# Setup of a two-direction graph attention kernel: key bursts over four PSUM banks become bursts over six, with a new order of the work between them

## The chip, the cores and the metric

The kernel runs on one core of one Trainium2 chip. The metric is device time in microseconds of one execution. TensorE is called PE here (PEld is its weight loading), VectorE DVE, ScalarE ACT, GpSimd POOL and SyncE SP. SP issues most DMAs, in the order of the program.

## The reference, cut to what matters

For each of B = 16 batches with N = 512 nodes and F = 512 features, each node attends, in two directions d, to the first 20 nodes of its batch, in 16 heads of 32 features:

```python
self_feat = concat([v, q_exp], -1) @ W_self.T + b_self
output = self_feat
for d in range(2):
    kv = self_feat[:, :20]
    qh = (self_feat @ Wq[d].T + bq[d]).reshape(B, N, 16, 32)
    kh = (kv @ Wk[d].T + bk[d]).reshape(B, 20, 16, 32)
    aff = einsum('bnhd,bmhd->bnhm', qh, kh) / sqrt(32)
    w = softmax(where(cond > 0, aff, NEG) + label_bias)
    out_t = einsum('bnhm,bmf->bnhf', w, kv)
    output = output + einsum('bnhf,hgf->bnhg', out_t, Wout[d]) + bout[d]
result = v + relu(output)
```

`cond` and `label_bias` are sums over 11 labels of an integer adjacency array, read one way for d = 0 and transposed for d = 1.

## The kernel before, in words

The kernel has a setup and a loop over the batches. All products are in fp32, and a matmul has two records in the trace, one for each of two passes. The order of the instructions is written out by hand on every engine (`manual_schedule`), so each engine and each DMA queue works through its own list in the order of the program.

**What setup makes.** It computes the features of the 20 attended nodes of all batches (`kvn`, 128 partitions by 4 blocks of features by 320), takes the first node of each batch from the other 19 (`kvD`, 16 x 19 = 304 columns, L822), and multiplies by Wk (`key_rows`, L839), which gives `khD`, one block of 304 columns for each direction d and group of four heads hg. Then `keys` (L938) multiplies each head's 32 rows of Wq with its `khD`, which turns the keys into vectors over the 512 features, so that the loop can take scores from `self_feat` alone. These are the **key bursts**. The whole is 4 blocks of features fc x 4 groups hg x 2 directions x 304 columns = 9,728 columns for each of four heads hl.

**A burst before.** The columns of a block stand as (batch, node). A burst takes 25 or 26 batches of 19 columns, 475 or 494 columns, in two or three runs, where a run ends at a change of fc, hg or d. The four heads hl lie on four groups of 32 partitions, so their matmuls (tile 32*128) run side by side, each into a PSUM bank of its own; two tiles of two banks, `ps_g..0` (heads 0 and 1) and `ps_g..1` (heads 2 and 3). ACT evicts the first pair (L960) and DVE the second (L962), both scaled, one instruction for each run, into the stage tile `st` of its (fc, hg). There are 20 bursts. Only one set of the four banks exists, so a burst begins when the last one's are evicted, and PE has other work in between, the **fillers**.

**Stages.** A stage tile holds both directions of one (fc, hg), 608 columns a head. Those of hg 0 to 2 share three buffers in turn, those of hg 3 have one. When a stage is full, POOL copies its first two batches to `gg` (L965) and SP writes the rest to DRAM (`g_d`, 1,064 KB, L968); both must be done before the buffer is used for a new stage.

**Fillers.** Letters in a plan name them:
- k: `key_rows` of a further (d, hg), four steps of four matmuls of 304 columns, with DVE's eviction to `khD` (L848)
- m: `bias_terms`, DVE alone (L856)
- b, c: `biases` (L862, L864) and `bias_scores` (L874: four matmuls of 304 columns, ACT's copy L879, POOL's addition L883 and four stores L885 to `cq_d`)
- v, w: one step k of `values` (L901): four matmuls of 512 columns, tiles of 128*32; after the fourth step `value_pieces` evicts on DVE (L917) and stores on POOL's queue (L921)
- n: `row_flags` (L220: four matmuls of 512 columns, then DVE L222)
- p: `block_product`, one of seven products (L282, 16 records of 246 columns) that give the first batch's `self_feat`, with DVE's `partial` (L295) or `joined` (L305)

Other work is placed by the number n of the burst: mask products, counts and sums of the first batch (`mask_mul` L321 and L322, `mask_count` L330 and L331, `mask_sum` L336, `mask_spread` L344), `row_sums` on POOL (L213, L215), `x_sum` on POOL (L255), `spill` (copies in DRAM from `vw_d` to `bd_d`, L191), and loads. `load_cq(0)` (L127) reads what both `bias_scores` have stored. The loop begins with `seed_a`, `seed_d` (L425, L429), which write to the banks of the last burst, and `score_product` (L395).

Of the kernel before, what the change touches and what calls it, by code (L numbers as in the profile page):

```python
# [18 lines left out]
def gat_kernel(  # L19
# [47 lines left out]
    def bank(name):  # L67
        return acc["pool"].tile([P, 512], F32, tag="acc", name=name)
# [188 lines left out]
    def product(b, n):  # L257

        w, x = {
            1: ((0, 0), lambda: x_block(b, 0, 0)),  # L260
            2: ((0, 1), lambda: x_block(b, 1, 0)),
            3: (3, lambda: x_block(b, 1, 1)),
            4: ((1, 1), lambda: sums[b, 4]),
            5: (0, lambda: sums[b, 1]),
            6: (1, lambda: sums[b, 2]),
            7: (2, lambda: sums[b, 3]),
        }[n]
        x = x()
        home = "d" if n == 2 else "c" if n in (3, 5) else "a"
        first, last = n in (1, 2, 5), n in (2, 3, 4)  # L270
        if first:
            parts[b, home] = bank(f"ps_{home}{b}")
        for i in range(2):
            for k in range(2):
                for a in range(2):
                    at = i * P + a * P // 2
                    if isinstance(w, tuple):
                        lhs = ws_v[:, 2 * w[1] + k, bass.ds(w[0] * F // 2 + at, P // 2)]
                    else:
                        lhs = ws_s[:, w, k, bass.ds(at, P // 2)]  # L280
                    to = parts[b, home][bass.ts(a, P // 2)]
                    nc.tensor.matmul(  # L282
                        to[:, bass.ts(i, HN)], lhs, x[:, k], start=first and i + k == 0,
                        stop=last and i + k == 2, skip_group_check=True,
                    )
# [411 lines left out]
    with tc.tile_pool(name="setup", bufs=1) as sp, tc.tile_pool(name="ps_acc", bufs=4, space=PSUM) as acc["pool"]:  # L697
# [18 lines left out]
        with tc.tile_pool(name="setup_k", bufs=1) as sk:  # L716
# [17 lines left out]
            warm = bank("ps_warm")  # L734
# [36 lines left out]
            load_x(1)  # L771
            load_adj(0, 1)
# [5 lines left out]
            kv_ps = [bank(f"ps_kv{fc}") for fc in range(C)]  # L778
# [32 lines left out]
            for fc in range(C):  # L811
# [11 lines left out]
                    kvD[:, fc].rearrange("p (b m) -> p b m", m=ND), each[:, :, 1:],  # L823
# [8 lines left out]
            def key_rows(d, jc, ks=range(C)):  # L832

                if ks[0] == 0 and (d, jc) not in of:
                    of[d, jc] = bank(f"ps_k{d}{jc}")
# [32 lines left out]
        with tc.tile_pool(name="setup_g", bufs=3) as sg:  # L868

            def bias_scores(d):  # L870

                ps = bank(f"ps_c{d}")
                for c in range(C):
# [7 lines left out]
                    ps[:, : B * ND].rearrange("p (b m) -> p b m", m=ND),  # L881
# [10 lines left out]
            def values(t, ds, k):  # L892
# [3 lines left out]
                if k == 0:  # L896
                    held[1 + t // 2] = bank(f"ps_v{t}{ds[0]}")
                ps = held[1 + t // 2]
                for i, d in enumerate(ds):
                    for a in range(rows // R):  # L900
                        nc.tensor.matmul(  # L901
                            ps[bass.ds(i * rows + a * R, R)], kvT[:, k, bass.ds(t * P + a * R, R)], wo_sb[d][:, k],
# [26 lines left out]
            def keys(runs):  # L929


                pairs = [ps_s.tile([P, 2, 512], F32, tag=f"s{i}", name=f"ps_g{runs[0]}{i}", bufs=1) for i in range(2)]
                at = 0
                for fc, hg, d, lo, hi in runs:
                    n = (hi - lo) * ND
                    for hl in range(HL):
                        r = bass.ts(hl, DH)
                        nc.tensor.matmul(  # L938
                            pairs[hl // 2][:, hl % 2, at : at + n], wq_sb[r, d, hg, bass.ts(fc, P)],
                            khD[r, d * C + hg, lo * ND : hi * ND], start=at == 0, stop=True, skip_group_check=True,  # L940
                        )
                    at += n
                if not units and runs is bursts[-1]:
                    for hl in range(HL):
                        r = bass.ts(hl, DH)
                        nc.tensor.matmul(
                            pairs[hl // 2][:, hl % 2, at:], wq_sb[r, 0, 0, :P], khD[r, 0, : 512 - at],
                            start=False, stop=True, skip_group_check=True,
                        )
                at = 0  # L950
                for fc, hg, d, lo, hi in runs:
                    n = (hi - lo) * ND
                    if (fc, hg) not in stages:
                        stages[fc, hg] = (late if hg == C - 1 else sg).tile([P, B, HL, 2, ND], F32, tag="st", name=f"st{fc}{hg}")
                    st = stages[fc, hg]
                    for half in range(2):
                        to = st[:, lo:hi, bass.ts(half, 2), d].rearrange("p b h m -> p h b m")
                        of = pairs[half][:, :, at : at + n].rearrange("p h (b m) -> p h b m", m=ND)
                        if half == 0:
                            nc.scalar.activation(to, of, AF.Copy, scale=SCALE)  # L960
                        else:
                            nc.vector.tensor_scalar(to, of, SCALE, None, ALU.mult)  # L962
                    at += n
                    if d == 1 and hi == B:
# [25 lines left out]
            plan = "mmvv bvv vvc vvc vvn vvw vw vw wn p p p p p p p".split()  # L990

            units = [(fc, hg, d, b) for fc in range(C) for hg in range(C) for d in range(2) for b in range(B)]
            bursts = []
            while units:
                runs = []
                for fc, hg, d, b in units[: 25 + (len(bursts) % 5 < 3)]:
                    if runs and runs[-1][:3] == (fc, hg, d):
                        runs[-1] = (*runs[-1][:4], b + 1)
                    else:
                        runs.append((fc, hg, d, b, b + 1))  # L1000
                del units[: 25 + (len(bursts) % 5 < 3)]
                bursts.append(runs)
            rest = [(d, hg) for hg in range(C) for d in range(2)]
            first = None
# [8 lines left out]
            for n, runs in enumerate(bursts):  # L1013
                for i in range(len(rest)):
                    if (i < 1 and n > 0) or any(fc == 0 and (d, hg) == rest[0] for fc, hg, d, _, _ in runs):
                        key_rows(*rest.pop(0))
                if n in (3, 4):
                    values(*steps["v"].pop(0)[1])
# [4 lines left out]
                keys(runs)  # L1023
                if n == 8:
                    mask_count(0, 0)
                if n == 14:
                    mask_count(0, 1)
                if n == 17:
                    mask_sum(0, 1)
                value_pieces()  # L1030
                if rest:
                    for kind in "mm" if n else ():
                        f, args = steps[kind].pop(0)
                        f(*args)
                    continue
                if n == 7:
                    mask_mul(0, 0)
                first = n if first is None else first
                for kind in plan[n - first] if n - first < len(plan) else ():
                    f, args = steps[kind].pop(0)  # L1040
                    f(*args)
                    if kind == "w":
                        value_pieces()
                if n == first:
                    for d in range(2):
                        nc.gpsimd.tensor_add(br_sb, br_sb, bo_rows[d])
                if n > first:
                    value_pieces()
                if n == 10:
                    mask_sum(0, 0)  # L1050
                    load_cq(0)
                if n == 9:
                    row_sums(1)
                    copies = blocks(0)
                if n > 13:
                    spill(1, nc.gpsimd)
                    spill(1)
                if n == 11:
                    mask_mul(0, 1)
                    new_self(0)  # L1060
                    for i in range(1, 5):
                        x_sum(0, i)
                if 10 < n < 15:
                    mask_spread(0, 0, (n - 11,))
                if n == 16:
# [3 lines left out]
                if n == 18:  # L1069
# [361 lines left out]
```

## Time and profile before

| | us |
|---|---|
| median of three runs (547.0 to 547.4) | 547.39 |
| the profiled execution | 547.86 |
| its span on the core | 546.2 |
| PE busy in the span | 539.7 |
| DVE, ACT, POOL busy | 482.4, 404.5, 451.0 |
| start of the first key burst | 24.25 |
| start of the loop's first score product | 89.86 |

The profile page gives, for one execution, each engine's busy time, the span in 40 slices, the DMA queues, the chain of work that ended last, the costliest groups of instructions and the DMA issues. A group's row has the source line, the engine, output and inputs, shape and count, then busy time and the mean of one, then the idle time ahead of it with what ended it. Ends of matmuls are modelled, so a busy PE is not PE at its peak. Where a number of the text is a time of day it counts from the start of the span.

### The profile page before, as it was taken

To read this page: it belongs to the slowest core of one execution; us is meant where nothing else is said; L and a number is where in the kernel's file an instruction comes from. 1 tells how busy PE (TensorE), PEld (TensorE's weight loads), DVE (VectorE), ACT (ScalarE), POOL (GpSimd) and SP (SyncE) were. 2 spreads that over 40 slices of the span, in tenths; PEclk is the share of its full clock that TensorE was granted. 3 is DMA by queue.
4 is the path that set the end of the run, shared out by engine and by line. 5 is a ranking of instruction groups with operands and counts; after the bars stand their busy time and mean duration, and the time that the engine had idled before them with its cause. 6 is when DMAs were issued, how large, how long until landed. Compare 5 with 4: busy or idle time off the path is not lost.

```text
span 546.2 us, 19842 instructions
## 1 busy us (share of the span) xinstructions
PE 539.7 (99%) x8012; PEld 421.6 (77%) x8012; DVE 482.4 (88%) x716; ACT 404.5 (74%) x1000; POOL 451.0 (83%) x454
## 2 busy tenths in 40 slices
PE   9999999999999999999999999999999999999996
PEld 5544368889888878787888878887878788878784
DVE  1786678889999999999989999999999999999997
ACT  1225436898887979888888888887878787978564
POOL 2557996779989797979898989898998979797675
PEclk9999999999999999999999999999999999999998
DMA  8998799656766867777766757575766676736025
GB/s 298 377 400 324 260 365 352 235 172 183 233 218 182 226 204 210 234 213 231 209 219 186 244 174 246 179 235 179 222 212 203 203 216 189 234 93 192 1 65 194
DMA packets 94603, 120.30 MB, mean 220 GB/s; under 512 B 19201, under 2 KB 62783, under 8 KB 92465
## 3 DMA queue, kind: packets, MB, share of 16 engines
q1 hardware_dynamic: 93088, 116.69, 66.6%
q0 software_dynamic: 992, 1.57, 1.4%
q8 instruction: 63, 1.03, 0.8%
q10 hardware_dynamic: 432, 0.79, 0.4%
q14 instruction: 28, 0.22, 0.1%
HBM read 83.41 MB, written 36.90 MB: 220 GB/s over the span
## 4 chain that ended last, share of the span: by engine, by line
PE 89%; DMA 4%; DVE 3%; SPq 1%; ACT 1%; issue 0%; POOL 0%; DVEq 0%; POOLq 0%; ACTq 0%
PE ps_f L665 32%; PE ps_a L395 24%; PE ps_c L395 11%; PE ps_d L395 6%; PE ps_o_f L567 5%; PE ps_v L901 2%; DMA wk<-in_wkT 2%; DMA wo<-in_woT 1%; PE ps_a L282 1%; PE ps_o_c L567 1%; DMA xkv<-in_xkvT 1%; PE ps_l L395 1%; DVE bqt L856 1%; PE ps_c L282 1%; DVE st L962 1%
## 5 line engine op out<-in xcount | busy, mean ns | idle before, releaser
L325 ACT ACTIVATE prod<-adj,wb_sb 128x80 f32<-128x80 int32 x330 | 116.1, 430 | 0.0
L535 POOL TENSOR_TENSOR w<-w,sm 128x640 f32<-128x640 f32 x63 | 80.2, 1273 | 30.5 <-DVE sm L531 28.7
L665 PE MATMUL ps_f<-t,ws_s 128*64 128x246 f32 x720 | 80.0, 370 | 0.0
L665 PEld LDWEIGHTS ps_f<-t,ws_s 128*64 128x64 f32 x720 | 51.7, 136 | 18.9
L526 ACT ACTIVATE w<-w 128x640 f32<-128x640 f32 x60 | 43.9, 731 | 17.9 <-DVE w L522 17.9
L543 DVE STREAM_TRANSPOSE wt<-w 128x640 f32<-128x640 f32 x63 | 52.5, 833 | 0.1
L665 PE MATMUL ps_f<-x,ws_v 128*64 128x246 f32 x480 | 52.4, 371 | 0.0
L530 DVE TENSOR_REDUCE sm<-w 128x32 f32<-128x640 f32 x63 | 51.1, 811 | 1.1 <-ACT w L526 0.9
L521 DVE TENSOR_REDUCE ps_d<-w 128x32 f32<-128x640 f32 x59 | 48.7, 826 | 1.8 <-ACT ps_d L429 0.2
L522 DVE TENSOR_TENSOR w<-w,ps_d 128x640 f32<-128x640 f32 x59 | 48.4, 820 | 2.0
L665 PEld LDWEIGHTS ps_f<-x,ws_v 128*64 128x64 f32 x480 | 34.7, 137 | 13.0
L368 POOL TENSOR_TENSOR k<-gg,k 128x608 f32<-128x608 f32 x30 | 44.6, 1487 | 0.0
L395 PEld LDWEIGHTS ps_a<-gg,sf 128*64 128x64 f32 x544 | 34.2, 137 | 5.9 <-issue 5.8
L395 PE MATMUL ps_a<-gg,sf 128*64 128x152 f32 x544 | 38.6, 295 | 0.0
L395 PE MATMUL ps_d<-gg,sf 128*64 128x152 f32 x544 | 37.9, 293 | 0.0
L336 DVE TENSOR_REDUCE add<-prod 128x80 f32<-128x960 f32 x32 | 36.7, 1146 | 0.2 <-POOL prod L331 0.2
L344 ACT COPY both<-add 64x80 f32<-64x80 f32 x128 | 32.6, 255 | 5.7 <-DVE add L336 4.6
L567 PE MATMUL ps_o_c<-wt,ve 32*32 32x256 f32 (+1 forms) x480 | 35.9, 386 | 0.0
L680 POOL TENSOR_TENSOR t<-x,t 128x492 f32<-128x492 f32 x30 | 34.9, 1162 | 1.2
L395 PEld LDWEIGHTS ps_d<-gg,sf 128*64 128x64 f32 x544 | 35.3, 137 | 0.2 <-ACT sf L683 0.2
L680 POOL TENSOR_TENSOR t<-x 128x492 f32<-128x492 f32 x30 | 34.5, 1149 | 0.0
L197 ACT ACTIVATE xn<-xn 128x512 f32<-128x512 f32 x56 | 34.5, 619 | 0.0
(310 smaller groups left out, 1490.9 us busy)
## 6 DMA issues: line engine op xcount, KB each, us to landing
g_d<-st SPq DMA_DIRECT2D x16, 1064.0 KB, 8.5
gg<-g_d SPq DMA_DIRECT2D x56, 304.0 KB, 3.1
out_T<-o SPq DMA_DIRECT2D x60, 256.0 KB, 2.8
x<-in_xT SPq DMA_DIRECT2D x56, 256.0 KB, 4.1
xn<-in_xn SPq DMA_DIRECT2D x48, 256.0 KB, 3.8
adj<-in_adj SPq DMA_DIRECT2D x52, 220.0 KB, 2.9
nz<-nz_d SPq DMA_DIRECT2D x14, 256.0 KB, 4.5
adj<-in_adj SPq DMA_DIRECT2D x6, 440.0 KB, 7.7
```

Of the source, the lines that this page charges most:

```text
L325: nc.scalar.activation(p[:, :, l], a[:, :, l], AF.Identity, scale=wb_sb[:, l : l + 1])
L368: done["ksum"] = engine.tensor_sub(to, one, two)
L395: nc.tensor.matmul(slot(g)[bass.ts(p, P // 2), : HL * S].rearrange("p (h m) -> p h m", m=NG)[:, :, 1:], of(k)[:, bass.ds(first + g * P // ...
L521: nc.vector.tensor_reduce(mx, f, AX.X, ALU.max)
L522: done["weigh"] = (engine or nc.vector).tensor_sub(f, f, mx.unsqueeze(2).to_broadcast([P, per, NG]))
L526: done["exp"] = nc.scalar.activation(t, t, AF.Exp)
L530: nc.vector.tensor_reduce(sm, heads(weighs[b, c, l]), AX.X, ALU.add)
L535: done["normal"] = nc.gpsimd.tensor_mul(f, f, smalls.pop((b, c, l)).unsqueeze(2).to_broadcast([P, per, NG]))
L543: done["turn"] = nc.vector.transpose(wts[b][:, c, l], weighs.pop((b, c, l)).rearrange("p g w -> p (g w)"))
L567: nc.tensor.matmul(outsum[b][a][bass.ds(at // 2 * DH, n * DH), bass.ds(c * N // 2 + lo * R, (hi - lo) * R)].rearrange("p (n r) -> p n r", ...
L665: nc.tensor.matmul(parts[b][n in (2, 3, 5)][bass.ts(a, P // 2), bass.ts(i, HN)], lhs, x[:, k], start=False, stop=k == 1, skip_group_check= ...
L680: done["xsum"] = nc.gpsimd.tensor_sub(to, one, two)
```

## The change

- The columns of `kvD`, and with it of `khD` and the bursts, now stand as (node, batch). A unit is one node of 16 columns (608 units), so that runs are cut at any node.
- A burst takes six banks: `ps_g..0` for heads 0 and 2 and `ps_g..1` for heads 1 and 3 take 30 to 32 units, 480 to 512 columns a head; two further banks (`t2`, "shared") take 11 or 16 units more, 256 columns of each of two heads in a bank. There are 13 bursts, all but one of 46 to 48 units. A matmul covers 96 columns or more.
- Even heads do their shared part first, odd heads last, so that no two heads write to one bank at a time; a `nop` on PE ahead of an odd head's shared part waits for the even head's. The matmuls of the four heads are issued in the order of the columns done so far.
- ACT evicts the shared part of all four heads and the own part of heads 0 and 2, DVE the own part of heads 1 and 3. A read from PSUM now steps by 16 columns, and the write in `st` is in runs of 6 to 19 nodes.
- The four accumulation banks in turn become two fixed ones, `acc0` and `acc1`, and the shared pair, which also serves two of the four `ps_kv`.
- `values` and `row_flags` use tiles of 64 columns, two matmuls where there were four.
- A new plan of the fillers by burst; `key_rows` are in it. Loads of the second batch and half a mask (`load_x(1)`, `load_adj(0, 1)`) go behind bursts 1 and 2 on SP's queue; all twelve early spills are on SP (six were on POOL's queue), two behind each of bursts 6 to 11; `row_sums(1)` is behind burst 5, `load_cq(0)` behind burst 7.
- The last burst's padding matmuls (L946) are gone.

The core of the diff:

```diff
-        ps = bank(f"ps_nz{b}")
-        for a in range(HL):
-            nc.tensor.matmul(ps[bass.ts(a, R), :N], ones[:, :R], rss[b], start=True, stop=True)
+        ps = bank(f"ps_nz{b}", 1)
+        for a in range(2):
+            nc.tensor.matmul(ps[bass.ts(a, P // 2), :N], ones[:, : P // 2], rss[b], start=True, stop=True)
...
-            load_x(1)
-            load_adj(0, 1)
...
-                    kvD[:, fc].rearrange("p (b m) -> p b m", m=ND), each[:, :, 1:],
+                    kvD[:, fc].rearrange("p (m b) -> p b m", b=B), each[:, :, 1:],
...
-                    for a in range(rows // R):
+                    for a in range(2 * rows // P):
                         nc.tensor.matmul(
-                            ps[bass.ds(i * rows + a * R, R)], kvT[:, k, bass.ds(t * P + a * R, R)], wo_sb[d][:, k],
+                            ps[bass.ds(i * rows + a * P // 2, P // 2)], kvT[:, k, bass.ds(t * P + a * P // 2, P // 2)], wo_sb[d][:, k],
...
+            def keys(n):
+
+                runs = bursts[n]
+                pairs = [ps_s.tile([P, 2, 512], F32, tag=f"s{i}", name=f"ps_g{n}{i}", bufs=1) for i in range(2)]
+                both = acc["pool"].tile([P, 2, 512], F32, tag="t2", name=f"ps_g{n}2")
+                each = [sorted(runs, key=lambda run: hl % 2 == run[5]) for hl in range(HL)]
+                gone = [0] * HL
+                while any(each):
+                    hl = min((hl for hl in range(HL) if each[hl]), key=lambda hl: gone[hl])
+                    fc, hg, d, lo, hi, more, at = each[hl].pop(0)
+                    r, w = bass.ts(hl, DH), (hi - lo) * B
+                    gone[hl] += w
+                    if more:
+                        to = both[:, hl // 2, bass.ds(hl % 2 * 256 + at, w)]
+                        if hl % 2 and at == 0:
+                            behind(nc.tensor.nop(), done["key", hl - 1])
+                    else:
+                        to = pairs[hl % 2][:, hl // 2, bass.ds(at, w)]
+                    one = nc.tensor.matmul(
+                        to, wq_sb[r, d, hg, bass.ts(fc, P)], khD[r, d * C + hg, lo * B : hi * B],
+                        start=at == 0 and not (more and hl % 2), stop=True, skip_group_check=True,
+                    )
+                    if more:
+                        done["key", hl] = one
...
+                def columns(t, at, n):
+                    return t[:, :, bass.ds(at, n * B)].rearrange("p h (m b) -> p h b m", b=B)
...
+                shared = both.rearrange("p c (u w) -> p (c u) w", u=2)
+                for *key, more, at in sorted(runs, key=lambda run: -run[5]):
+                    to, w = stage(*key), key[4] - key[3]
+                    if more:
+                        nc.scalar.activation(to, columns(shared, at, w), AF.Copy, scale=SCALE)
+                    else:
+                        nc.vector.tensor_scalar(to[:, 1::2], columns(pairs[1], at, w), SCALE, None, ALU.mult)
+                        nc.scalar.activation(to[:, ::2], columns(pairs[0], at, w), AF.Copy, scale=SCALE)
...
-            plan = "mmvv bvv vvc vvc vvn vvw vw vw wn p p p p p p p".split()
+            plan = "kmmk kmmmk mmmvvv vvv vvvb cvvv vvvc vnw www np pp pp pp".split()
...
+            for own_n, both_n, swap in [(30, 16, 0), (30, 11, 0), (30, 16, 1)] + [(31, 16, 0), (32, 16, 1)] * 5:
+                bursts.append([])
+                for more in (swap, 1 - swap):
+                    n = both_n if more else own_n
...
+                if n == 1:
+                    load_x(1)
+                if n == 2:
+                    load_adj(0, 1)
...
+                if n == 5:
                     row_sums(1)
                     copies = blocks(0)
+                if n == 6:
+                    mask_sum(0, 0)
+                if 5 < n < 12:
+                    spill(2)
+                if n == 7:
+                    load_cq(0)
                     mask_mul(0, 1)
                     for i in range(1, 5):
                         x_sum(0, i)
```

More of the change, by code (lines that the diff above doesn't have):

```diff
@@ L65, in gat_kernel, with bank @@
     acc = {}
-    def bank(name):
-        return acc["pool"].tile([P, 512], F32, tag="acc", name=name)
+    def bank(name, i):
+        return acc["pool"].tile([P, 512], F32, tag=f"acc{i}", name=name)
     ctx.enter_context(tc.manual_schedule())
@@ L271, in product @@
         if first:
-            parts[b, home] = bank(f"ps_{home}{b}")
+            parts[b, home] = bank(f"ps_{home}{b}", int(home != "a"))
         for i in range(2):
@@ L693, in self_lift @@
             )
-    with tc.tile_pool(name="setup", bufs=1) as sp, tc.tile_pool(name="ps_acc", bufs=4, space=PSUM) as acc["pool"]:
+    with tc.tile_pool(name="setup", bufs=1) as sp, tc.tile_pool(name="ps_acc", bufs=1, space=PSUM) as acc["pool"]:
         wq_sb = sp.tile([P, 2, C, F], F32, name="wq_sb")
@@ L733, in gat_kernel @@
                 )
-            warm = bank("ps_warm")
+            extra = acc["pool"].tile([P, 2, 512], F32, tag="t2", name="ps_kv")
+            warm = extra[:, 1]
             for _ in range(6):
@@ L777, in gat_kernel @@
                 nc.gpsimd.tensor_add(rsk, rsk, xkv[:, k])
-            kv_ps = [bank(f"ps_kv{fc}") for fc in range(C)]
+            kv_ps = [*(bank(f"ps_kv{fc}", fc) for fc in range(2)), extra[:, 0], extra[:, 1]]
             def kv_terms(fc, k, w=R):
@@ L834, in key_rows @@
                 if ks[0] == 0 and (d, jc) not in of:
-                    of[d, jc] = bank(f"ps_k{d}{jc}")
+                    of[d, jc] = bank(f"ps_k{d}{jc}", d)
                 ps = of[d, jc]
@@ L870, in bias_scores @@
             def bias_scores(d):
-                ps = bank(f"ps_c{d}")
+                ps = bank(f"ps_c{d}", 1)
                 for c in range(C):
@@ L896, in values @@
                 if k == 0:
-                    held[1 + t // 2] = bank(f"ps_v{t}{ds[0]}")
+                    held[1 + t // 2] = bank(f"ps_v{t}{ds[0]}", int((t, ds) == (0, (1,))))
                 ps = held[1 + t // 2]
                 for i, d in enumerate(ds):
-                    for a in range(rows // R):
+                    for a in range(2 * rows // P):
                         nc.tensor.matmul(
-                            ps[bass.ds(i * rows + a * R, R)], kvT[:, k, bass.ds(t * P + a * R, R)], wo_sb[d][:, k],
+                            ps[bass.ds(i * rows + a * P // 2, P // 2)], kvT[:, k, bass.ds(t * P + a * P // 2, P // 2)], wo_sb[d][:, k],
                             start=(k == 0), stop=(k == C - 1),
@@ L927, in gat_kernel @@
             nc.gpsimd.memset(stages["c"][:, :, :BM], 0.0)
[L929 to L952, printed above, removed]
@@ new lines, in keys, with stage @@
+            def keys(n):
[21 more added lines that the diff above has]
+                        done["key", hl] = one
+                def stage(fc, hg, d, lo, hi):
@@ L953, in keys @@
                     if (fc, hg) not in stages:
                         stages[fc, hg] = (late if hg == C - 1 else sg).tile([P, B, HL, 2, ND], F32, tag="st", name=f"st{fc}{hg}")
[L955 to L962, printed above, removed]
@@ L963, in keys @@
-                    at += n
-                    if d == 1 and hi == B:
+                    return stages[fc, hg][:, :, :, d, lo:hi].rearrange("p b h m -> p h b m")
+                def columns(t, at, n):
+                    return t[:, :, bass.ds(at, n * B)].rearrange("p h (m b) -> p h b m", b=B)
+                for *key, _, _ in runs:
+                    stage(*key)
+                shared = both.rearrange("p c (u w) -> p (c u) w", u=2)
[6 more added lines that the diff above has]
+                        nc.scalar.activation(to[:, ::2], columns(pairs[0], at, w), AF.Copy, scale=SCALE)
@@ L965, in keys @@
+                for fc, hg, d, lo, hi, *_ in runs:
+                    if d == 1 and hi == ND:
+                        st = stages[fc, hg]
                         nc.gpsimd.tensor_copy(
@@ L989, in gat_kernel @@
             }
-            plan = "mmvv bvv vvc vvc vvn vvw vw vw wn p p p p p p p".split()
[L992 to L1002, printed above, removed]
+            plan = "kmmk kmmmk mmmvvv vvv vvvb cvvv vvvc vnw www np pp pp pp".split()
+            units = [(fc, hg, d, m) for fc in range(C) for hg in range(C) for d in range(2) for m in range(ND)]
+            bursts, lo = [], 0
+            for own_n, both_n, swap in [(30, 16, 0), (30, 11, 0), (30, 16, 1)] + [(31, 16, 0), (32, 16, 1)] * 5:
+                bursts.append([])
+                for more in (swap, 1 - swap):
+                    n = both_n if more else own_n
+                    for i, (fc, hg, d, m) in enumerate(units[lo : lo + n]):
+                        if i and m:
+                            bursts[-1][-1][4] = m + 1
+                        else:
+                            bursts[-1].append([fc, hg, d, m, m + 1, more, i * B])
+                    lo += n
             rest = [(d, hg) for hg in range(C) for d in range(2)]
-            first = None
             for rs, ks in (((0, 2), (0, 1)), ((1, 3), (0, 1)), ((0, 1), (2, 3)), ((2, 3), (2, 3))):
@@ L1012, in gat_kernel @@
             del rest[:4]
[L1013 to L1018, printed above, removed]
+            for n in range(len(bursts)):
                 if n == 0:
@@ L1022, in gat_kernel @@
                         nc.sync.dma_start(bo_rows[d], bout[d : d + 1].partition_broadcast(P))
-                keys(runs)
-                if n == 8:
+                keys(n)
+                if n == 1:
[3 more added lines that the diff above has]
+                if n == 5:
                     mask_count(0, 0)
-                if n == 14:
+                if n == 9:
                     mask_count(0, 1)
-                if n == 17:
+                if n == 10:
@@ L1029, in gat_kernel @@
                     mask_sum(0, 1)
[L1030 to L1040, printed above, removed]
+                for kind in plan[n]:
+                    f, args = (key_rows, rest.pop(0)) if kind == "k" else steps[kind].pop(0)
@@ L1041, in gat_kernel @@
                     f(*args)
-                    if kind == "w":
-                        value_pieces()
-                if n == first:
+                    value_pieces()
+                if n == 2:
                     for d in range(2):
                         nc.gpsimd.tensor_add(br_sb, br_sb, bo_rows[d])
[L1047 to L1052, printed above, removed]
+                if n == 3:
+                    mask_mul(0, 0)
@@ L1062, in gat_kernel @@
                         x_sum(0, i)
-                if 10 < n < 15:
-                    mask_spread(0, 0, (n - 11,))
-                if n == 16:
+                if n == 8:
+                    new_self(0)
+                if 6 < n < 9:
+                    mask_spread(0, 0, (2 * n - 14, 2 * n - 13))
+                if n == 10:
                     gs.update((b, gg[:, b]) for b in range(2))
@@ L1068, in gat_kernel @@
                     load_adj(1, 0)
-                if n == 18:
+                if n == 11:
                     mask_spread(0, 1)
```

8 lines of the change are left out of this document (2 added, 6 removed).

## The prediction

> **What bounds the kernel now.** I read the page first (chain and span), then busy time by window to split setup from loop, then the TensorE timeline and the chain in order of time inside setup, and last the forms of the evicting instructions and the timelines of POOL and SP.
>
> ```profile
> span 546.2 us, 19842 instructions
> PE 89%; DMA 4%; DVE 3%; SPq 1%; ACT 1%; issue 0%; POOL 0%; DVEq 0%; POOLq 0%; ACTq 0%
> ```
>
> ```profile
> 24.25:89.92 65.67, 65.29 (x842) 33.90 (x840) 47.65 (x92) 28.06 (x67) 47.60 (x65) 1.00 0.94 337
> 89.92:546.20 456.28, 451.31 (x6905) 374.50 (x6904) 424.92 (x602) 372.37 (x927) 391.84 (x371) 1.00 0.64 197
> ```
>
> The columns are length, then busy time of PE, PEld, DVE, ACT and POOL, the clock, the DMA share and GB/s. The chain is TensorE's. From the first key burst (24.25) to the loop's first score product (89.86) PE is busy 65.29 of 65.67 us while DVE, ACT and POOL have room (47.65, 28.06, 47.60); the loop behind it is PE's too, at clock 1.00. So what PE is spared in setup should come off the end one to one, if no engine is made late. The profiled execution took 547.86 us, 1.66 outside its span; the runs' median is 547.39, 0.47 below it. I take differences within the span and subtract them from 547.39.
>
> **PE's sum.** What is a burst worth, beyond its columns?
>
> ```profile
> 24.25 0.52 PE L938 MATMUL s_g(0, 0, 0, 0, 16)0_378<-khD,wq_sb 32*128 32x304 f32 x2
> ...
> 60.27 0.53 PE L938 MATMUL s_g(2, 0, 0, 0, 16)0_776<-khD,wq_sb 32*128 32x304 f32 x2
> ...
> 61.31 1.92 PE L901 MATMUL ps_v<-wo,kvT 128*32 128x512 f32 x16
> 63.16 0.37 PE L938 MATMUL _g(2, 0, 1, 10, 16)0_805<-khD,wq_sb 32*128 32x114 f32 x2
> ...
> 66.14 0.46 PE L938 MATMUL s_g(2, 1, 1, 4, 16)0_850<-khD,wq_sb 32*128 32x228 f32 x2
> ...
> 89.86 2.29 PE L395 MATMUL ps_a<-gg,sf 128*64 128x152 f32 x32
> ```
>
> ```profile
> 57.62 2.71 PE ps_v L901 x24
> ...
> 61.38 1.85 PE ps_v L901 x16
> ...
> 76.10 1.81 PE ps_a L282 x16
> ```
>
> Three value steps take 2.71 and two take 1.85, so one is 0.86: 512 columns, two passes, all column groups side by side, 0.84 ns per column and pass. At that rate the keys (9,728 columns per head, two passes, four heads side by side) are 16.3 us; four key_rows 8.2; sixteen v and four w steps 17.2; two row_flags 1.7; two bias_scores 1.0; seven block products 11.6 (1.65 of columns each, the 1.81 row has the switch in it). Sum 56.0 of 65.6: **9.6 us are bursts' overhead**, 0.48 for each of 20. The change leaves every column where it is. Tiles of 64 columns two abreast move as many columns as of 32 four abreast, so `values` and `row_flags` gain nothing of size.
>
> How the 0.48 splits decides. The burst of 60.27 (two runs, 494 columns, two v steps) takes 2.89 to the next start: less 0.83 and 1.72, 0.34. That of 63.16 (three runs, same columns) takes 2.98: 0.43. If the 0.09 belongs to the 76-column run, a burst of runs of 96 and more costs 0.36; if each run costs it, the new bursts of four runs cost 0.52. By the loops there are 48 runs now and 51 then. Thirteen bursts at 0.36 to 0.52 are 4.7 to 6.8; two fillers of 32-wide tiles now stand against 64-wide ones, twice 0.15 (1.81 less 1.65). So **PE is spared 2.5 to 4.6 us; I take 3.0**, near the end that charges each run, because the four heads no longer run in step. The last burst's padding (37 columns, 0.06) is in that. The added waits of PE on its own even heads can release 0.43 us into a burst (256 columns, two passes), while the odd heads behind them need that at 0.80 (480 columns): hidden while a release takes under 0.37. Were it to take the 0.52 of the row at 24.25, it would be 0.15 a burst, 2.0 in all; the odd heads' shared part and whatever run is issued after it would stand behind the wait.
>
> **The evictions.**
>
> ```profile
> L960 ACT ACTIVATE st<-_g(0, 0, 1, 10, 16)0_411 128x608 f32<-128x608 f32 x1 | 0.7, 690 | 0.0
> ...
> L960 ACT ACTIVATE st<-_g(0, 0, 1, 10, 16)0_411 128x152 f32<-128x152 f32 x1 | 0.3, 304 | 0.0
> ```
>
> ```profile
> L962 DVE TENSOR_SCALAR st<-_g(0, 0, 1, 10, 16)1_412 128x608 f32<-128x608 f32 x1 | 0.8, 781 | 0.0
> ...
> L962 DVE TENSOR_SCALAR st<-_g(0, 0, 1, 10, 16)1_412 128x152 f32<-128x152 f32 x1 | 0.3, 305 | 0.0
> ```
>
> Slopes: ACT 0.85 ns an element, DVE 1.04. A full burst gives ACT 1,024 shared and 992 own elements in four instructions, about 2.1 us, and DVE 992 in two, 1.3. The cover is the filler: three v steps, 2.6, and even heads need their own banks only 0.43 after the burst's start. So eviction is **hidden at these slopes**, by 0.9 us. But the new columns stand (m b) in PSUM and are read with a step of 16 floats; before they were read in order. No row has such a read from PSUM. The nearest is a stepped read and write in SBUF:
>
> ```profile
> L325 ACT ACTIVATE prod<-adj,wb_sb 128x80 f32<-128x80 int32 x330 | 116.1, 430 | 0.0
> ```
>
> ```profile
> L626 ACT ACTIVATE ps_f<-nz,qw 128x246 f32<-128x246 f32 x30 | 14.1, 470 | 15.4 <-DVE o L584 14.7 <-DVE sf L305 0.2
> ...
> L321 ACT CAST prod<-adj 128x880 f32<-128x880 int32 x2 | 1.9, 935 | 0.0
> ```
>
> L626, in order and with the same scale operand, would take 330 for 80 elements; L325 takes 430: 1.25 ns an element more, a factor of 2.5. The integer input is not the cause (L321: 935 for 880 is the plain slope). So the read costs between 0 and 1.25 ns an element more. I take 0: that row steps on both sides, in SBUF, and here the write stays in runs. [...]
>
> `kvD` is now written with that step, four times, ahead of key_rows:
>
> ```profile
> L822 DVE TENSOR_TENSOR kvD<-kvn 128x304 f32<-128x304 f32 x4 | 3.3, 831 | 0.1
> ```
>
> At nothing it is hidden; at 1.25 ns it adds 0.4 each, and PE starts its first key_rows 0.4 later, the others being behind PE's pace.
>
> **What is late next.** Fillers, POOL and SP are closer packed. With 0.5 a burst the starts come to: burst 5 at 48.6, 7 at 58.5, 8 at 62.8, 10 at 71.4, 11 at 76.6, loop 86.9.
>
> ```profile
> 56.99 0.72 POOL L883 TENSOR_TENSOR c<-c,bb_sb 128x320 f32<-128x320 f32 x1
> 58.01 2.51 POOL L885 DMA_DIRECT2D cq_d<-c  x4 [0.29 <-POOL c L883]
> 60.51 0.45 POOL L965 COPY gg<-st 128x304 f32<-128x304 f32 x1
> 61.05 0.57 POOL L331 TENSOR_SCALAR prod<-cond 128x80 f32<-128x80 f32 x1
> 61.68 0.86 POOL L921 DMA_DIRECT2D vw_d<-v  x1
> ...
> 62.95 1.27 POOL L213 TENSOR_TENSOR rx<-x 128x512 f32<-128x512 f32 x1
> 64.30 2.64 POOL L215 TENSOR_TENSOR rx<-rx,x 128x512 f32<-128x512 f32 x2
> ...
> 68.07 2.11 POOL L322 TENSOR_TENSOR prod<-prod,wb_sb 128x880 f32<-128x880 f32 x1
> 70.12 1.06 POOL L255 TENSOR_TENSOR t<-x 128x492 f32<-128x492 f32 x1
> ...
> 73.54 1.15 POOL L255 TENSOR_TENSOR t<-x,t 128x492 f32<-128x492 f32 x1
> ...
> 79.67 0.63 POOL L191 DMA_DIRECT2D bd_d<-vw_d  x1
> ```
>
> ```profile
> 65.53 2.25 SPq L127 DMA_DIRECT2D cq<-cq_d  x2
> 67.89 6.91 SPq L968 DMA_DIRECT2D g_d<-st  x4
> ```
>
> ```profile
> GB/s 298 377 400 324 260 365 352 235 172 183 233 218 182 226 204 210 234 213 231 209 219 186 244 174 246 179 235 179 222 212 203 203 216 189 234 93 192 1 65 194
> ...
> g_d<-st SPq DMA_DIRECT2D x16, 1064.0 KB, 8.5
> ```
>
> Now the second bias score leaves POOL at 60.5, ahead of row_sums(1), and SP stands until 65.5 for it before `load_cq(0)`, then writes the next stage. In the new order row_sums(1) (3.9) is ahead of it. POOL begins burst 5's copy when ACT is done, 52.3; copy and count 1.0, first bias score 3.5, a value store 0.8, row sums 3.9, copy 0.5, second bias score 3.5: 65.5. Five us of landing, as now, and `load_cq(0)` starts at 70.5 and is issued by 72.8. Behind them in SP's queue is the write of stage (2,1), ready since 65; its buffer is wanted by burst 10's last eviction at 73.5 (three buffers, reused in turn). The write takes between 2.7 us (1.06 MB at the 400 GB/s that the page reaches) and the 8.5 of the row: it lands between 75.5 and 81.3; as SP sent nothing for some six us before it, I take 76.8, the lower end and 1.3 to issue it. DVE's 608 elements then end at 77.6, and burst 11 starts 1.1 late (0 to 5.5). Queued behind that eviction on DVE are
>
> ```profile
> 62.80 1.14 DVE L336 TENSOR_REDUCE add<-prod 128x80 f32<-128x960 f32 x1
> ...
> 72.15 0.85 DVE L295 SCALAR_TENSOR_TENSOR sf<-nz,qw,ps_a 128x246 f32<-128x246 f32 x2 [0.49 <-PE ps_a L282]
> 75.31 0.66 DVE L305 TENSOR_TENSOR sf<-ps_d,sf 128x492 f32<-128x492 f32 x1
> ```
>
> 2.65 together, to 80.2; product 7 writes the bank that the L295 pair reads, and is wanted at 79.2: 1.0 more. If the store were not late, POOL's backlog (product mask 2.1 and four sums of x, 4.6, to 73.6, then copies, stores and the count at 76.8) would hold the mask sum alone and cost 1.4. Sum: 3.0 spared, 2.1 given back, 0.1 for the value bank that w reuses: **0.8, so 546.6**. Moving `load_x(1)` and `load_adj(0,1)` behind SP's stage writes costs nothing: they land before bursts 5 and 7. Twelve spills leave POOL for SP (six of about 0.7), which is in the sums above.
>
> **Rivals.**
> - *Nothing is late.* The cq store or the stage write lands early enough. PE keeps 3.0, up to 4: 543.4 to 545.9, middle 544.4. For it: ACT and DVE are half idle in setup. Against: SP's order is plain in the two SP rows.
> - *Stage writes later still.* The write takes the median 8.5: burst 11 is 5 late, 1.0 behind: 3.0 less 6.0 less 0.1, 550.5; halfway 549.
> - *Stepped PSUM reads cost* (the slower end). At twice 0.85, ACT's burst is 3.4 + 0.4. A period is then 1.5 + 3.8 + 0.2 - 0.43 = 5.1 against 4.3 in six bursts, 4.9 in two: 5.2 late in all, and after the last burst 3.8 + 0.2 and a seed (0.7) stand against 3.5 of filler, 1.2 more: 550.8 after 3.0 spared, the stage write being hidden behind it. At 2.5 times, period 5.9, about 559. It decides from 0.45 ns an element, where 0.9 of slack is gone.
> - *Heads out of step.* If four matmuls had to end before the next four begin, 768 columns become 1,024: 0.43 a burst, 5.6 in all, 549.9. Against: the order by columns issued is meant for heads that run apart; no row has such heads.
> - *The change does not do what it says*: columns and evictions are all there by the loops; only the mix of runs is open, and that is the 2.5 to 4.6.
>
> **How the numbers follow.** Forecast as worked out (545.9 to 547.8) 32 in 100; nothing late 30; stage writes later 13; stepped reads 16; heads out of step 6; other 3. Faster by over 0.2% (below 546.3; about what a measurement can tell from none) is all of the second and a third of the first: 0.41. Within it: the rest of the first and some of the third, 0.28. Slower 0.31. The range leaves out the upper part of stepped reads and the lowest tail: 543.6 to 550.8; the forecast's own is 545.9 to 547.8.
>
> **What would show it.** Burst starts: 13 at 4.2 to 5.2 us; a burst's PE time 1.5 to 1.6; the loop at 86 to 88. ACT's 128x608 form at 690 or well above it says whether stepped reads cost, at once. SP's cq row near 70 and a gap on DVE's last eviction of burst 10, ended by a DMA, show the stage write; its absence with the loop at 86 makes the second case. The forecast is wrong if the loop does not begin before 89, or if a loop begun early meets a wait in its first 20 us.

## The result, and the profile after

The changed kernel takes **553.47 us** (median of four runs, 552.4 to 554.57) beside 547.35 for the kernel before: a ratio of 1.0113, 95% interval 1.009 to 1.0136. It is slower by 6 us, outside the predicted range. The profiled execution took 554.07.

The page of the kernel after, its span and then the chain that ended last, by engine:

```profile
span 552.0 us, 19653 instructions
PE 93%; POOL 3%; DVE 2%; issue 1%; ACT 0%; DVEq 0%; POOLq 0%; ACTq 0%
```

POOL, 0% of the chain before, now has 3%, 17 us. Next the busy time by window of the kernel after (length, then busy time of PE, PEld, DVE, ACT and POOL, the granted clock, DMA share, GB/s): from the first burst to the loop's first score product, product 7, product 5, and the loop.

```profile
24.45:94.59 70.14, 65.76 (x767) 38.43 (x765) 39.34 (x70) 34.21 (x70) 44.03 (x60) 0.95 0.93 337
83.59:86.89 3.30, 3.30 (x16) 2.14 (x18) 1.01 (x2) 0.40 (x2) 0.92 (x2) 0.50 0.94 302
86.89:89.45 2.56, 2.56 (x18) 1.52 (x14) 0.85 (x2) 0.00 (x0) 0.00 (x0) 0.69 0.99 351
94.59:552.00 457.41, 451.50 (x6910) 377.42 (x6906) 423.48 (x602) 372.20 (x927) 390.88 (x370) 1.00 0.64 193
```

The stretch before the loop was 65.61 long and now is 70.14: 4.53 of the 5.8 by which the span grew. The first burst starts 0.20 later (in the kernels of the experiments, with the same work ahead of it, at 23.56 to 24.79), and the loop took 1.07 longer, with PE busy 451.50 in it where it was 451.31. Two things are in the 70.14: PE stands 4.4 us where it stood 0.4, and its clock is at 0.50 and 0.69 right behind that. The TensorE timeline of the kernel after (start, length, instruction; in brackets idle time and what ended it) shows where:

```profile
75.56 1.88 PE L282 MATMUL ps_a<-t,ws_s 128*64 128x246 f32 x16 [0.30 <-POOL t L255]
77.38 0.47 PE L946 MATMUL ps_g<-khD,wq_sb 32*128 32x112 f32 x2
79.06 1.66 PE L946 MATMUL ps_g<-khD,wq_sb 32*128 32x304 f32 x30 [1.21 <-DVE st L969]
83.59 3.55 PE L282 MATMUL ps_a<-t,ws_s 128*64 128x246 f32 x16 [2.87 <-DVE sf L295]
86.89 2.63 PE L282 MATMUL ps_c<-t,ws_s 128*64 128x246 f32 x16
```

Up to the end of burst 10 the view shows no wait. Then product 6 waits 0.30 for a sum of x, burst 11 1.21 for DVE's eviction, and product 7 2.87 for DVE's `partial`. Why DVE is late is read from its own timeline, and from POOL's:

```profile
78.21 0.80 DVE L969 TENSOR_SCALAR st<-ps_g 128x608 f32<-128x608 f32 x1 [4.82 <-POOL gg L974]
80.95 1.15 DVE L336 TENSOR_REDUCE add<-prod 128x80 f32<-128x960 f32 x1 [1.95 <-POOL prod L331]
```

```profile
62.16 1.27 POOL L213 TENSOR_TENSOR rx<-x 128x512 f32<-128x512 f32 x1 [4.03 <-PE ps_nz L220]
63.50 2.62 POOL L215 TENSOR_TENSOR rx<-rx,x 128x512 f32<-128x512 f32 x2
...
67.47 2.51 POOL L884 DMA_DIRECT2D cq_d<-c  x4 [0.29 <-POOL c L882]
...
76.66 1.14 POOL L255 TENSOR_TENSOR t<-x,t 128x492 f32<-128x492 f32 x1
77.74 0.82 POOL L974 COPY gg<-st 128x304 f32<-128x304 f32 x2
...
80.36 0.56 POOL L331 TENSOR_SCALAR prod<-cond 128x80 f32<-128x80 f32 x1
```

DVE waits 4.82 for POOL's copy of a full stage to `gg`, then 1.95 for POOL's mask count. And POOL stood 4.03 from 58.1, before `row_sums(1)`, for `row_flags(0)` on PE. Both batches' row sums come from one pair of buffers (tag `xn`), which three tiles share: `rx0` and `rx1` (the row sums of batches 0 and 1) and `c` (the bias scores). Here `rx1` gets the buffer of `rx0`, which `row_flags(0)` still has to read. PE's row of it in the kernel before, then in the kernel after:

```profile
55.57 1.04 PE L220 MATMUL ps_nz<-rx,ones 128*32 128x512 f32 x8
```

```profile
61.03 1.03 PE L220 MATMUL ps_nz<-rx,ones 128*64 128x512 f32 x4
```

Before, it had run at 55.57, some seven us ahead of `row_sums(1)` (62.95); the new plan puts it at 61, in burst 7's fillers, and `row_sums(1)` behind burst 5. The chain of the page goes from `row_flags(0)` through POOL's row sums, stores, sums of x, copies and mask count to DVE's mask sum and `partial`, and from there to product 7.

**Theory T**: that wait on the shared buffer is the root; POOL is 4 us late from there on, its copies are late, DVE's and ACT's evictions with them, PE stands, and the clock falls. **Rival S**: SP's order, as the prediction had it (`load_cq(0)` ahead of the stage writes). **Rival B**: POOL simply has too much in front of its copies, wait or no wait.

### The profile page after: what moved, and what is told of

It is laid out like the page before. It is cut to its first block, busy times and chain, and to the rows that moved or that the text cites. A ratio compares the mean times of both kernels' runs of the same rounds, so it can differ in the third digit from the quotient of the medians.

```text
span 552.0 us, 19653 instructions
## 1 busy us (share of the span) xinstructions
PE 540.4 (98%) x7940; PEld 428.8 (78%) x7940; DVE 473.1 (86%) x694; ACT 410.5 (74%) x1003; POOL 447.0 (81%) x448
## 4 chain that ended last, share of the span: by engine, by line
PE 93%; POOL 3%; DVE 2%; issue 1%; ACT 0%; DVEq 0%; POOLq 0%; ACTq 0%
PE ps_f L665 32%; PE ps_a L395 24%; PE ps_c L395 11%; PE ps_d L395 6%; PE ps_o_f L567 5%; PE ps_k L838 3%; PE ps_v L900 3%; PE ps_g L946 2%; PE ps_kv L781 2%; PE ps_o_c L567 1%; PE ps_a L282 1%; PE ps_l L395 1%; PE ps_c L282 1%; PE ps_kv L737 1%; POOL t L255 0%
## 5 line engine op out<-in xcount | busy, mean ns | idle before, releaser
L967 ACT ACTIVATE st<-ps_g 128x448 f32<-128x448 f32 (+5 forms) x25 | 14.8, 643 | 35.5 <-PE ps_g L946 23.9
```

## The experiments

The first four kernels, the next three and the last three were measured on three different chips, each time beside the kernel before, whose medians there are 547.49, 547.42 and 547.17; medians of different groups compare to some 0.3 us.

**One tile for both row sums** (own_rx). It takes away the wait and moves nothing:

```diff
-        t = rss[b] = load.tile([P, 2, F], F32, tag="xn", name=f"rx{b}")[:, 0]
+        if b == 0:
+            rss["rx"] = load.tile([P, 2, F], F32, tag="xn", name="rx")
+        t = rss[b] = rss["rx"][:, b]
```

> Kernel after, but the row sums of batches 0 and 1 share one tile (its two halves), so POOL's row_sums(1) needs no buffer back and the order of all work stays. Theory T (the wait of 4.03 us on POOL for row_flags(0) is the root): POOL stands nowhere from 58 to 74, the copies of stages (2,1) and (2,2) to gg come at 73 to 74.5 instead of 77.74, PE idles under 0.8 us in all before product 7 instead of 4.9, the clock stays at 1.00, the loop starts at 87 to 88 and the time is 545.0 to 547.0. Rival S (SP's order, load_cq(0) ahead of the stage writes, sets the buffer free): the stage write still lands 3 to 5 us after its data were ready, PE idles 2 to 3 us and the time is 549 to 551. Rival B (POOL simply has too much in front of the copies): copies still at 75 or later, 548 to 551.

Measured: 547.6 us, ratio to before 0.9998 (0.9988 to 1.0008). POOL's and then DVE's and PE's timelines of this kernel:

```profile
57.96 1.28 POOL L215 TENSOR_TENSOR rx<-x 128x512 f32<-128x512 f32 x1
...
73.56 0.82 POOL L976 COPY gg<-st 128x304 f32<-128x304 f32 x2
```

```profile
74.67 0.79 DVE L971 TENSOR_SCALAR st<-ps_g 128x608 f32<-128x608 f32 x1 [1.45 <-DMA g_d<-st]
76.77 1.15 DVE L338 TENSOR_REDUCE add<-prod 128x80 f32<-128x960 f32 x1 [1.31 <-POOL prod L333]
```

```profile
79.40 1.89 PE L284 MATMUL ps_a<-t,ws_s 128*64 128x246 f32 x16 [1.15 <-DVE sf L297]
```

The row sums start with no wait, the copies come 4.2 earlier (73.56 for 77.74), the clock stays at 1.00, and 5.9 us of the 6.1 lost are back. That is T. But T had PE idle under 0.8 and a time of 545.0 to 547.0; PE idles 1.15, the time is 0.6 above that range, and the two DVE rows name what is left: the stage write (S) and the mask count (B).

**Row sums moved instead** (rows_later): `row_sums(1)` from behind burst 5 to behind burst 7, the buffers shared as they were.

> Kernel after, but row_sums(1) is issued behind burst 7's fillers (behind row_flags(0)) instead of behind burst 5; the shared buffer stays. T: the wait goes as in the run before; the second bias score's addition and stores leave POOL at 58 to 61 instead of 66.5 to 70, the copies of stages (2,1) and (2,2) come at 72.5 to 74, the loop starts at 87 to 88, time 544.8 to 546.8. S: 548 to 550, since SP's load_cq(0) is early but the writes behind it are no faster. B: 548 to 551, POOL having as much work ahead of the copies as before.

Measured: 552.3, ratio 1.0079 (1.0065 to 1.0093): above what was written for T, S and B alike. POOL and PE:

```profile
60.51 2.50 POOL L884 DMA_DIRECT2D cq_d<-c  x4 [0.29 <-POOL c L882]
...
68.79 1.26 POOL L213 TENSOR_TENSOR rx<-x 128x512 f32<-128x512 f32 x1 [4.61 <-issue]
```

```profile
72.79 1.98 PE L220 MATMUL ps_nz<-rx,ones 128*64 128x512 f32 x4 [3.50 <-POOL rx L215]
74.55 3.50 PE L282 MATMUL ps_a<-x,ws_v 128*64 128x246 f32 x16
```

Issued that late, `rx1` gets the buffer of `c`, whose last use now stands ahead of that of `rx0` in the program, and waits for the bias scores' stores: the last is issued at 63.0, POOL goes on at 68.79. (The row names no releaser; the view of tile `c` lists `rx` L213 as waiting 4.6 for it, and the last store lands at 68.49.) The second `row_flags`, a filler of burst 9, then holds PE for 3.50. The shared pair of buffers makes the wait in either place. The clock falls here too, to 0.50 from 72 to 76 (product 1 takes 3.50 where it takes 1.83 in after), at another place and with another wait.

**`load_cq(0)` later** (cq_later): SP's load behind burst 9 instead of 7, nothing else.

> Kernel after, but SP's load_cq(0) is issued behind burst 9 instead of 7, so that the stage writes of bursts 7 to 9 go ahead of it. T: POOL's wait and its late copies are as they were, the time is 552.5 to 554.5, PE's idle time before product 7 still 4 to 5 us. S: SP no longer stands from 64.7 to 70.2, PE's idle time falls to 2 or less and the time to 547.5 to 550.

Measured: 552.83, ratio 1.0092 (1.0078 to 1.0107); product 7 still waits 2.86. In the kernel after, SP's order sets nothing of size: the median is 0.64 lower, with runs that overlap (551.57 to 553.54, and 552.4 to 554.57). POOL is later than SP.

**POOL's work spread** (reordered): `row_sums(1)` behind burst 7; `load_cq(0)`, the mask product and two sums of x behind burst 8; the other two sums behind burst 9.

> Kernel after, but POOL's work is spread: row_sums(1) behind burst 7, load_cq(0), the second mask product and two sums of x behind burst 8, the other two sums behind burst 9. T: no wait on POOL, copies to gg within 2 us of each full stage, PE idle under 0.4 us before product 7, loop at 86.8 to 87.5, time 543.8 to 545.8, below both kernels. S: 547 to 550. B: 544 to 546 as well, but then the run with row_sums(1) alone moved stays at 548 or more.

Measured: 550.13, ratio 1.0055 (1.0041 to 1.007), far above T's 543.8 to 545.8, by the same fault as rows_later: `rx1` has the buffer of `c` again, and the second `row_flags` waits 3.38 for POOL's row sums.

**What the shared tile leaves.** Three runs on top of own_rx part S from B: `load_cq(0)` behind burst 9 (own_cq), sums 3 and 4 of x behind burst 9 (own_split), and both (own_split_cq).

```diff
-                if n == 7:
+                if n == 9:
                     load_cq(0)
+                if n == 7:
                     mask_mul(0, 1)
-                    for i in range(1, 5):
+                    for i in range(1, 3):
                         x_sum(0, i)
+                if n == 9:
+                    for i in range(3, 5):
+                        x_sum(0, i)
```

> The run with one tile for both row sums, and load_cq(0) issued behind burst 9 instead of 7. What is left in that run is 1.15 us of idle PE before product 7, behind DVE's chain mask sum, joined, partial. If SP's order still sets this (S: DVE's eviction of burst 10 waits for the stage write until 74.67), the eviction begins 1 us or more earlier and PE's idle time falls to 0.3 or less, loop start 87.1, 545 to 546.8. If POOL's order sets it (B: the mask count is behind four sums of x, copies and stores, to 76.73), the eviction begins earlier, but the mask sum still starts at 76.7, PE idles 1.0 to 1.2 and the time is that of the run before, 547.0 to 548.2.

> The run with one tile for both row sums, and POOL's sums 3 and 4 of x issued behind burst 9 (behind the mask count) instead of burst 7. B: the mask count ends at 74 to 75 instead of 76.73, the mask sum follows DVE's eviction at 75.5, PE idles 0.3 or less before product 7, loop start 86.9 to 87.2, 544.8 to 546.9. S: the mask sum still waits behind DVE's eviction, held by the stage write until 74.67, and PE idles 0.5 to 1.

> Both edits of the two runs before on one tile for both row sums. PE waits for nothing from the first burst to the loop, which begins at 86.9 (the change's PE time spared, 3.0, in full); time 544.0 to 546.3, below the kernel before. If the loop itself is longer in these kernels than before (456.3 in its profile), the time stays at 547 although the loop begins 3 us earlier.

Measured: 546.04 (0.998, 0.9971 to 0.9989), 546.93 (0.9996, 0.9986 to 1.0007) and **545.57 (0.9968, 0.9957 to 0.9979)**. DVE and PE of own_cq, then DVE and PE of own_split:

```profile
76.36 1.15 DVE L338 TENSOR_REDUCE add<-prod 128x80 f32<-128x960 f32 x1 [1.95 <-POOL prod L333]
```

```profile
79.00 1.89 PE L284 MATMUL ps_a<-t,ws_s 128*64 128x246 f32 x16 [1.17 <-DVE sf L297]
```

```profile
76.33 0.79 DVE L971 TENSOR_SCALAR st<-ps_g 128x608 f32<-128x608 f32 x1 [3.50 <-DMA g_d<-st]
```

```profile
77.17 1.66 PE L948 MATMUL ps_g<-khD,wq_sb 32*128 32x304 f32 x30 [0.51 <-DVE st L971]
79.66 1.88 PE L284 MATMUL ps_a<-t,ws_s 128*64 128x246 f32 x16 [0.83 <-DVE sf L297]
```

With SP mended, POOL's mask count sets the end, and PE idles 1.17, as B had it; but the time, 546.04, is below what I had written for B and inside what I had written for S. With POOL mended, the stage write behind `load_cq(0)` sets it: the eviction waits 3.50 and PE 0.51 + 0.83 = 1.34, more than the 0.5 to 1 written for S. Each mends one of two late paths of about the same length, so in the profiles neither alone brings PE anything: from the first burst to the loop it is 63.75 in own_rx, 63.76 in own_cq and 64.40 in own_split. The medians say otherwise of SP: own_cq's is 1.6 below own_rx's, and the two ratios' intervals barely touch. The profiles do not explain this. own_rx's profiled run was the fastest of its eleven (546.27), so the stage write may be later in its usual runs than in its rows; no trace shows one of them, and it stays open. With both, the windows from the first burst to the loop and from there to the end are:

```profile
23.78:86.30 62.52, 62.52 (x767) 36.86 (x765) 39.94 (x70) 33.97 (x70) 43.97 (x60) 1.00 1.00 358
86.30:542.80 456.50, 451.71 (x6910) 377.47 (x6906) 423.32 (x602) 372.15 (x927) 390.47 (x370) 1.00 0.66 197
```

PE is busy in the whole of it, and 62.52 is 3.09 below the 65.61 of before. By the medians this version is 1.85 us faster than the kernel before. Its burst 11, product 7 and product 5 are the scale for the slower ones elsewhere:

```profile
76.09 1.66 PE L948 MATMUL ps_g<-khD,wq_sb 32*128 32x112 f32 x32
77.68 1.88 PE L284 MATMUL ps_a<-t,ws_s 128*64 128x246 f32 x16
79.40 1.83 PE L284 MATMUL ps_c<-t,ws_s 128*64 128x246 f32 x16
```

**The wait put back** (split_cq): the same two moves, with the buffers shared as in after.

> Kernel after with the two moves (load_cq(0) behind burst 9, sums 3 and 4 of x behind burst 9), but with the buffer shared as in after: the best run so far less its tile for both row sums. T: POOL still stands 4.0 us before row_sums(1), the two copies to gg come at 76.3 and the mask count at 78.7, so that product 7 starts near 81.3: PE idles 2.5 to 3.2 us, loop start 89 to 91.5, time 548 to 551.5. If the wait alone matters little once the rest is in order, the time is 545 to 546.5.

Measured: 550.13, ratio 1.0046 (1.0033 to 1.0059). POOL waits 4.04 for `row_flags(0)` again. POOL, then PE:

```profile
61.86 1.27 POOL L213 TENSOR_TENSOR rx<-x 128x512 f32<-128x512 f32 x1 [4.04 <-PE ps_nz L220]
```

```profile
80.97 3.51 PE L282 MATMUL ps_a<-t,ws_s 128*64 128x246 f32 x16 [2.25 <-DVE sf L295]
84.22 1.98 PE L282 MATMUL ps_c<-t,ws_s 128*64 128x246 f32 x16
```

With 0.29 before product 6, PE idles 2.54 in all, and the clock falls over product 7 (0.63 from 80 to 84; 3.51, for 1.88 in own_split_cq). Against own_split_cq the shared buffer costs 4.6 us in the medians, with the order of SP and POOL mended; with the order as in after it cost 5.9 (own_rx). T stands; S and B are the second layer, worth 1.2 in the profiles and 2.0 in the medians (own_rx to own_split_cq).

**What idle time costs** (sums_2, sums_4). From own_split_cq, DVE's second mask sum is computed three and five times (into the same result; the diff is that of sums_2, sums_4 has 4 for its 2), which holds back what product 7 waits for and leaves the other engines' work as it is:

```diff
+        for _ in range(2 if (b, h) == (0, 1) else 0):
+            nc.vector.tensor_reduce(add, prods[b, h], AX.X, ALU.add)
         done["masks"] = nc.vector.tensor_reduce(add, prods.pop((b, h)), AX.X, ALU.add)
```

> The best run so far with DVE's second mask sum computed three times instead of once (same result), which holds DVE 2.2 us longer ahead of the adds that product 7 waits for; 1.1 of it is slack in that run's rows (0.48 before the adds, 0.63 from their end to product 7). Only this idle time of PE is added: 1.1 us, loop start 87.4, time 546.4 to 547.0. Were a short stand enough to lower the granted clock, products 7 and 5 would take over 1.9 each and the time would be over 548.

> As the run before, with the second mask sum computed five times: 4.4 us more on DVE, 3.3 of idle PE before product 7. If idle time costs only itself: 548.6 to 549.2, clock 0.997. If the clock falls after it, as it did in after (products 7 and 5 at 3.55 and 2.63 instead of 1.88 and 1.83, 2.5 us): 550.5 to 551.5 and a mean clock of 0.990 to 0.994, in all or in most of the runs.

Measured: 546.0 (0.9983, 0.9974 to 0.9992) and 550.64 (1.006, 1.0043 to 1.0077). PE of sums_2, then of sums_4:

```profile
79.29 1.88 PE L284 MATMUL ps_a<-t,ws_s 128*64 128x246 f32 x16 [1.24 <-DVE sf L297]
80.97 1.86 PE L284 MATMUL ps_c<-t,ws_s 128*64 128x246 f32 x16
```

```profile
81.15 3.55 PE L284 MATMUL ps_a<-t,ws_s 128*64 128x246 f32 x16 [3.62 <-DVE sf L297]
84.46 2.90 PE L284 MATMUL ps_c<-t,ws_s 128*64 128x246 f32 x16
```

1.24 us of idle time cost itself and no clock (1.00 from 72 to 92): from the first burst to the loop 63.84, 1.32 above own_split_cq (0.4 in the medians; the 546.0 is below the 546.4 to 547.0 that I had written). 3.62 cost 6.35 there (5.1 in the medians): itself, and 2.65 for the slower products behind it (3.31 and 2.82 from start to start, for 1.72 and 1.76 in own_split_cq). The six runs of sums_4 had mean clocks of 0.990 to 0.997; the one at 0.997 took 548.4, 3.6 above own_split_cq's profiled run (544.8) and 2.8 above its median: about the idle time alone.

## Why the prediction was wrong

**PE is spared 3.0: right.** own_split_cq, where PE waits for nothing, gives 3.09 in its profile; own_rx 63.75 less its wait of 1.15, 3.0. Of the 3.09, 0.38 are waits that PE had there in the kernel before (0.16 and 0.22); its work fell by 2.71, inside the 2.5 to 4.6. Bursts of four runs do cost about what charging each run gave: 62.52 less the 56.0 of columns leaves 6.5, for 6.6 in the forecast (9.6 less 3.0).

**Evictions hidden, stepped reads at nothing: right.** By forms, of the kernel after:

```profile
L970 ACT ACTIVATE st<-ps_g 128x608 f32<-128x608 f32 x13 | 9.2, 705 | 3.2 <-POOL gg L974 3.2
L969 DVE TENSOR_SCALAR st<-ps_g 128x608 f32<-128x608 f32 x13 | 10.2, 787 | 11.0 <-PE ps_g L946 5.0 <-POOL gg L974 4.8 <-ACT bqbd L863 1.2
L821 DVE TENSOR_TENSOR kvD<-kvn 128x304 f32<-128x304 f32 x4 | 4.1, 1030 | 0.1
```

The reads that step by 16 floats in PSUM take 705 for 690 and 787 for 781. The row that I had put at the far end (1.25 ns an element more) steps in SBUF; the one stepped write in SBUF that the change has, `kvD`, did cost 0.2 each, inside the 0 to 0.4. So the rival of stepped reads falls, and so does that of heads out of step: a burst of 46 to 48 units takes 1.46 to 1.60 from its start to the next instruction's in own_split_cq, for 1.5 to 1.6 forecast. No run shows the factor of two on which the 550.8 of the first of them rests: these reads from PSUM take 15 and 6 ns more, of some 700 and 780.

**SP's order gives back 2.1: right in mechanism, but second in line.** own_split shows it alone: DVE's eviction held by the stage write, burst 11 0.51 late and product 7 0.83, 1.34 for the forecast's 1.1 + 1.0; with 0.53 more for the burst that the wait splits, PE loses 1.88 to own_split_cq before the loop. That it comes so near is partly luck: the load that delays the write went at 68.85 and not at 70.5, and the write, issued at 70.14, released DVE only 6.2 later, at 76.33, for 4.0 in the forecast. In after this path is hidden (cq_later: nothing of size gained). The forecast's other price, 1.4 for POOL's backlog behind the mask sum alone, is own_cq's 1.17. The sum began on five us of landing between POOL's last `cq_d` store and SP's load. `load_cq(0)` is two loads, and each waits for two of POOL's four stores. The last store landed 7.4 us after its issue began in before (59.90 to 67.27), 4.4 in own_split and only 2.1 in after (69.36 to 71.50), where the loads went at 70.20 and 71.55. So SP's row "near 70", one of the signs in the prediction, came true by luck: POOL's stores left 4.5 later than forecast and landed sooner.

**The step that failed** is in "What is late next": "row sums 3.9", added to POOL's work right behind a value store at 57. I placed the instruction and counted its time, but didn't ask whose buffer it writes. The row of before had shown it with no wait because `row_flags(0)` was long done; in the new order it stands two bursts ahead of `row_flags(0)`, in POOL's queue, with 15.6 us of POOL's work from its start (62.16) to the copies (77.74). A wait of 4.03 stood where the sum had none, and none of the rivals had it either. It took the backlog's end from 73.6, as forecast, to 77.74, PE's idle time from 2.1 to 4.38 (0.30, 1.21 and 2.87), and the clock fell to 0.50 in the last of these waits.

**The clock was not in the sum.** Products 7 and 5 took 3.30 and 2.56 from start to start, 2.38 more than in own_split_cq. With 0.54 more for the split burst 11 (3.34 with its wait of 1.21, for 1.59; own_split, at clock 1.00, has the same) and 0.15 on burst 10, the stretch adds up: -3.09 + 4.38 + 2.38 + 0.54 + 0.15 = 4.36, of 4.53 measured.

Two things stay open. The loop of after was 1.07 longer than that of before in the one profile of each; the other kernels' loops took 456.2 to 456.9, and no wait of PE in the loop tells them apart. And own_split_cq keeps 3.4 us of span in the profiles, but 1.85 in the medians: its profiled run was one of its fastest (544.8), before's one of its slower ones; and some 0.3 more lies outside the span (2.0 for 1.66).

## What to carry to other kernels

When an instruction is moved on an in-order queue, ask which buffer it writes and who still reads that buffer at the new time; no row of the old profile shows a wait that the old order had satisfied. A move can also change which buffer it gets, as in rows_later. Then price the wait by all that is queued behind it, not by its own instruction. When several engines are nearly late at the same place, mending one shows the next, so a mend whose profile shows no gain may still be needed; and PE's idle time can cost more than itself: 1.24 us (sums_2) did not, 3.62 (sums_4) did.

## What the hardware showed that I had not expected

The granted clock after idle time of PE, by window, of sums_4 (columns as above; product 7 starts at 81.15):

```profile
76.00:80.00 4.00, 1.53 (x32) 1.25 (x32) 3.90 (x5) 2.36 (x5) 1.96 (x3) 0.97 0.86 305
80.00:84.00 4.00, 2.85 (x14) 1.91 (x16) 2.17 (x5) 0.78 (x4) 0.92 (x2) 0.50 1.00 354
84.00:88.00 4.00, 4.00 (x36) 2.65 (x36) 1.46 (x3) 0.00 (x0) 0.00 (x0) 0.68 0.94 293
88.00:92.00 4.00, 4.00 (x56) 3.30 (x50) 2.20 (x5) 2.92 (x6) 1.11 (x3) 1.00 0.50 193
```

With idle times of 2.87 (after), 2.86 (cq_later), 3.50 (rows_later) and 3.62 (sums_4) the clock in the profiles was at 0.50 for some 6.8 us, by the windows; in after from 81.6, 0.9 into the idle time, to 88.5. With 2.25 (split_cq) it was at 0.63 and 0.94 in the windows from 80 to 84 and from 84 to 88, as 3.4 us at 0.50 would give. With 1.15 (own_rx) and 1.24 (sums_2) it did not move from 1.00. It does not happen each time: reordered's profiled run kept 1.00 through 3.38 idle (product 1 at 1.83, mean clock 0.998, 548.54 us), and its five other runs had 0.990 to 0.995 and 549.91 to 552.18. What decides it, these runs do not show.
